# Clipping a block's tap results on VectorE instead of ScalarE, in a deformable bottleneck followed by a batch-norm bottleneck

## The chip, the cores and the metric

The kernel runs on one core of a Trainium2 chip. The metric is the device time of one execution in microseconds; lower is better. TensorE (PE in the profile), VectorE (DVE), ScalarE (ACT) and GpSimd (POOL) each work through a queue of instructions in order, and SyncE (SP) issues most of the DMAs. PEld is TensorE's loading of weights, which overlaps its matmuls.

## The reference, cut to what matters

```python
def _L0_conv_ref(x, w1, b1, w_off, b_off, w2, b2, w3, b3):     # x: (4, 1024, 56, 56) float32
    r = jax.nn.relu(_conv(x, w1, b1))                          # 1x1, 1024 -> 256
    r = jax.nn.relu(_deform_conv3x3(r, w2, b2, w_off, b_off))  # 9 taps, 256 -> 256
    r = _conv(r, w3, b3)                                       # 1x1, 256 -> 1024
    return jax.nn.relu(x + r)

def _deform_conv3x3(feat, w, b, w_off, b_off):
    off = _conv(feat, w_off, b_off)                            # an offset for each pixel and tap
    ...
    sampled = _bilinear_gather(feat, ys.reshape(n, -1), xs.reshape(n, -1))
    out = jnp.einsum('nckhw,ock->nohw', sampled, w.reshape(w.shape[0], c, K))
    return out + b[None, :, None, None]
```

A second bottleneck follows (1x1, 3x3 and 1x1 convolutions with batch norm over all images), and its result is added to its input. The change lies in the first one: in the bias `b` and the relu behind `_deform_conv3x3`.

## The kernel before, in words

All data is float32. An image of 56 x 56 pixels is cut into seven blocks of 512, 512, 512, 512, 384, 384 and 320 pixels (`SIZES`), so four images have 28 blocks, and a block has nine taps.

**The tap stage** (about 210 to 2050 us of the span) is one loop over the 252 taps of all blocks. In each turn of the loop, three things are recorded for three different taps:

- `sample`, two taps ahead: for each 128 pixels, GpSimd issues an indirect DMA that gathers four neighbours (L509), ScalarE scales the first (L519) and VectorE adds the other three (L521). The gathered tiles `g` have eight buffers.
- `turn`, one tap ahead: TensorE transposes the sampled pixels (L546), ScalarE copies them out of PSUM (L552) and VectorE makes three differences (L554, L555, L556). These feed a product of 2 x 2 blocks in seven multiplications.
- `tap`: the seven matmuls (L574), summed over the nine taps in four banks of PSUM.

Behind a block's ninth tap, `tap` copies the seven sums out with five instructions on ScalarE (L589 to L593) and joins them with seven additions on VectorE (L595 to L601). The result is `r2`, a tile of two halves of 128 channels with a row of the block's pixels each. One turn of the loop later, `clip_taps` adds the bias and applies the relu on ScalarE, in place, one instruction for each half (L609), and puts the block on the list `last_ones`.

What is left of TensorE's time in a turn goes to other stages, as generators that give way after each piece: `stage_a` of a later image (first 1x1 convolution L331, seeds L283, offsets L421, the table for the gathers L394) and `stage_c` of a finished block taken from `last_ones`. `stage_c` seeds a bank with the input (L632, ScalarE), multiplies `r2` (L636), applies the relu into `x1t` (L647, ScalarE) and feeds that into the first convolution of the second bottleneck (seeds L283 and L658, matmuls L662, copy out L672). A budget of TensorE columns per turn decides how much of these is recorded behind each tap. A scheduler then settles each engine's own order; an engine executes that order strictly.

For the last image, a further generator, `filters`, prepares the second bottleneck's 3x3 weights on VectorE (L724 to L736 and L777). Behind the tap stage come the 3x3 convolution (to about 2380 us) and the last 1x1 convolution with the output (to the end).

Of the kernel before, what the change touches and what calls it, by code (L numbers as in the profile page):

```python
# [10 lines left out]
AF = mybir.ActivationFunctionType  # L11
ALU = mybir.AluOpType
# [4 lines left out]
KB = CB // 128  # L17
# [17 lines left out]
SIZES = (512, 512, 512, 512, 384, 384, 320)  # L35
# [26 lines left out]
def deform_bottleneck_then_bn_bottleneck(  # L62
# [15 lines left out]
    nc = tc.nc  # L78
# [25 lines left out]
    def col(name, k):  # L104
        c = COLS[name] + k
        return ch[:, c : c + 1]
# [66 lines left out]
    with ExitStack() as l0:  # L173
# [327 lines left out]
        samples, turned, accs, r2s = {}, {}, {}, {}  # L501

        def sample(n, j, k):

            size = SIZES[j]
            for t in range((size + 127) // 128):
                m = min(128, size - t * 128)
                g = gat.tile([128, 4 * CB], F32, tag="g", name=f"g_{n}_{j}_{k}_{t}")
                nc.gpsimd.indirect_dma_start(  # L509
                    out=g[:m],  # L510
                    out_offset=None,
                    in_=tables[n].rearrange("r q c -> r (q c)"),
                    in_offset=bass.IndirectOffsetOnAxis(
                        ap=idxs[n, j][:m, t, k : k + 1], axis=0
                    ),
                )
                s = w3p.tile([128, CB], F32, tag="s", name=f"s_{n}_{j}_{k}_{t}", bufs=8)
                wt = wts[n, j][:m, :, t, k : k + 1]
                nc.scalar.activation(s[:m], g[:m, 0:CB], AF.Copy, scale=wt[:, 0])  # L519
                for corner in range(1, 4):  # L520
                    nc.vector.scalar_tensor_tensor(  # L521
                        s[:m],
                        g[:m, corner * CB : (corner + 1) * CB],
                        wt[:, corner],
                        s[:m],
                        ALU.mult,
                        ALU.add,
                    )
                samples[n, j, k, t] = s

        def turn(n, j, k):

            size = SIZES[j]
            half = size // 2
            sts = w3p.tile([128, 7, 256], F32, tag="sts", name=f"sts_{n}_{j}_{k}", bufs=2)
            banks = [
                ps1.tile([128, 512], F32, tag="bank", name=f"stp_{n}_{j}_{k}_{h}")
                for h in range(KB)  # L540
            ]
            for t in range((size + 127) // 128):
                m = min(128, size - t * 128)
                s = samples.pop((n, j, k, t))
                for h in range(KB):
                    nc.tensor.transpose(  # L546
                        banks[h][:, t * 128 : t * 128 + m],
                        s[:m, h * 128 : (h + 1) * 128],
                        ident[:m, :m],
                    )  # L550
            for h, to in ((0, sts[:, 0:3:2, :half]), (1, sts[:, 3:5, :half])):
                nc.scalar.copy(to, banks[h][:, :size].rearrange("p (e q) -> p e q", e=2))  # L552
            t1, t2 = sts[:, 2, :half], sts[:, 1, :half]
            nc.vector.tensor_sub(t1, t1, sts[:, 0, :half])  # L554
            nc.vector.tensor_sub(t2, sts[:, 4, :half], t1)  # L555
            nc.vector.tensor_sub(sts[:, 5:7, :half], sts[:, 1:4:2, :half], sts[:, 0:2, :half])  # L556
            turned[n, j, k] = sts
# [4 lines left out]
        def tap(n, j, k):  # L562
            size = SIZES[j]
            half = size // 2
            if k == 0:
                accs[n, j] = [
                    pst.tile([128, 512], F32, tag=f"tap{i}", name=f"acc2_{n}_{j}_{i}")
                    for i in range(4)
                ]
            sts = turned.pop((n, j, k))  # L570
            sums = [accs[n, j][i // 2][:, i % 2 * half : (i % 2 + 1) * half] for i in range(7)]
            for i, (a, b) in enumerate(PRODUCTS):

                nc.tensor.matmul(  # L574
                    sums[i],
                    w2[:, a, k],
                    sts[:, b, :half],
                    start=(k == 0 and i % 2 == 0),
                    stop=(k == TAPS - 1),
                    skip_group_check=True,  # L580
                )
            if k == TAPS - 1:
                r2 = work.tile([128, KB, 512], F32, tag="r2", name=f"r2_{n}_{j}", bufs=R2S)
                p3, p5, p4 = (
                    w3p.tile([128, CB], F32, tag="p", name=f"p{i}_{n}_{j}", bufs=3)[:, :half]
                    for i in (3, 5, 4)
                )
                r = [[r2[:, o, e * half : (e + 1) * half] for e in range(2)] for o in range(KB)]
                nc.scalar.copy(r2[:, 0, :size], accs[n, j][0][:, :size])  # L589
                nc.scalar.copy(p3, sums[2])  # L590
                nc.scalar.copy(p5, sums[3])
                nc.scalar.copy(r2[:, 1, :size], accs[n, j][2][:, :size])
                nc.scalar.copy(p4, sums[6])  # L593
                add = nc.vector.tensor_add
                add(r[1][0], r[1][0], r[0][0])  # L595
                add(r[1][1], r[1][1], r[1][0])
                add(r[0][0], r[0][0], r[0][1])
                add(r[0][1], r[1][0], p5)
                add(r[0][1], r[0][1], p3)
                add(r[1][0], r[1][1], p4)  # L600
                add(r[1][1], r[1][1], p5)  # L601
                r2s[n, j] = r2

        def clip_taps(n, j):

            size = SIZES[j]
            r2 = r2s[n, j]
            for o in range(KB):
                nc.scalar.activation(  # L609
                    r2[:, o, :size], r2[:, o, :size], AF.Relu, bias=col("a_b2", o)  # L610
                )
            last_ones.append((n, j))

        def stage_c(n, j):

# [85 lines left out]
        def last_positions(n):  # L701
            for j in range(NJ - positions_behind(n), NJ):
                yield from stage_b(n, j)
# [271 lines left out]
        last_ones = []  # L975
# [29 lines left out]
        stage, upcoming, extra, done, budget = None, None, None, None, 0.0  # L1005
        for i, (n, j, k) in enumerate(taps):
            if i + 1 < len(taps):
                turn(*taps[i + 1])
            nxt = next(ahead, None)
            if nxt is not None:  # L1010
                sample(*nxt)
            tap(n, j, k)
            if done is not None:
                clip_taps(*done)
            done = (n, j) if k == TAPS - 1 else None
            if (j, k) == (0, 0):
                waiting = last_positions(n) if n else None

            if waiting and k % 2 == 0:
                next(waiting, None)  # L1020
            if (n, j, k) == (N - 1, 1, 0):
                l0a.close()
                extra = filters()
            if extra and k:
                next(extra, None)
            budget += share * SIZES[j]
            passed = (STARTS[j] + SIZES[j] * k / TAPS) / HW
            while budget > 0 or due(n, j, k):
                if stage is None:
                    stage = upcoming  # L1030
                    if stage is None:
                        stage = next_stage(n, j, passed)
                        if stage is None:
                            break
                    else:
                        upcoming = None
                cost = next(stage, 0)
                if cost == LAST:
                    upcoming = next_stage(n, j, passed)
                    if upcoming is not None:  # L1040
                        next(upcoming)
                elif cost == 0:
                    stage = None
                elif cost in (None, BEGUN):
                    if not due(n, j, k):
                        break
                else:
                    budget -= cost
        clip_taps(*done)
        while last_ones or stage or upcoming:  # L1050
            if stage is None:
                if upcoming is None and len(last_ones) == 1:
# [19 lines left out]
    with l1:  # L1072
# [37 lines left out]
        size = (HALF + 2) * KB * W  # L1110
# [291 lines left out]
        for i, p in [(i, p) for i in range(len(parts)) for p in SEQ] + [(len(parts), None)]:  # L1402
            begun = begin(i, p) if p is not None else None
            if before is not None:
                j, q, _ = before
# [71 lines left out]
    with ExitStack() as l2:  # L1477
# [45 lines left out]
        done = 1  # L1523
        before = None
        for i in range(0, len(chunks), 2):
            n, at, m = chunks[i + 1]
# [92 lines left out]
    def add(t, k, e, ps):  # L1619
        to = t[:, e * BLK : (e + 1) * BLK]  # L1620
        nc.vector.scalar_tensor_tensor(to, ps, sc3[:, k : k + 1], to, ALU.mult, ALU.add)  # L1621
# [170 lines left out]
```

## Time and profile before

| what | value |
|---|---|
| time of the runs, median of 3 | 2801.86 us (2799.9 to 2802.9) |
| the profiled execution's own time | 2791.22 us |
| its span, first to last instruction | 2789.4 us |
| mean granted TensorE clock | 0.992 of full speed |
| busy: TensorE, VectorE, ScalarE, GpSimd | 2722.1, 2183.5, 1496.3, 1169.8 us |
| L609, the clip on ScalarE | 56 instructions, 545 to 752 ns each |
| L521, VectorE's sums of samples | 2700 instructions, 1173.8 us |

A group of instructions is named by line, engine, operation and `out<-in` tiles, with its shape and count, then its busy time in us, the mean of one in ns, and the idle time of the engine just before it with what ended that. A wait reads "engine tile line <- who ended it: total us, times, longest us". A row of the timeline gives start, duration, engine, line, operation, tiles and count; in brackets stands the idle time before it and its releaser. A row of windows gives a stretch of the span and each engine's busy time in it.

### The profile page before, as it was taken

How to read it: one execution, taken by the hardware profiler on the slowest of the kernel's cores; microseconds unless marked ns; L12 is line 12 of the kernel's file. 1: busy time of each engine (PE TensorE's matmuls, PEld its weight loads, DVE VectorE, ACT ScalarE, POOL GpSimd, SP SyncE). 2: the span in 40 equal slices, each digit the busy share in tenths (PEclk: the TensorE clock that was granted, in tenths of full speed). 3: DMA queues.
4: the chain of work that ended last, by engine and by line, in shares of the span. 5: the costliest groups of instructions: out<-in, count | busy, mean ns of one | idle time of the engine just before them, and what ended most of it. 6: DMA issues, size and time to landing. Idle time of an engine off the chain costs nothing.

```text
span 2789.4 us, 39697 instructions
## 1 busy us (share of the span) xinstructions
PE 2722.1 (98%) x12045; PEld 1927.4 (69%) x12045; DVE 2183.5 (78%) x5199; ACT 1496.3 (54%) x3045; POOL 1169.8 (42%) x1054
## 2 busy tenths in 40 slices
PE   9989999999999999999999999999989999999999
PEld 7656666777666676667676666667769999864554
DVE  5488888888788889877788989878759988337777
ACT  2345656565545655556565656666643444524444
POOL 0166554565665466556555656554500000111111
PEclk9999999999999999999999999999999999999999
DMA  8699999999999999999998989999831110219998
GB/s 291 203 344 387 367 350 327 314 338 353 352 334 349 349 291 350 314 344 369 338 345 278 375 296 351 343 368 341 269 123 38 36 43 5 95 60 341 347 346 304
DMA packets 313318, 792.70 MB, mean 284 GB/s; under 512 B 33768, under 2 KB 134672, under 8 KB 313104
## 3 DMA queue, kind: packets, MB, share of 16 engines
q0 software_dynamic: 127296, 462.48, 46.6%
q1 hardware_dynamic: 167376, 276.30, 28.7%
q10 hardware_dynamic: 18432, 51.39, 4.7%
q8 instruction: 95, 1.56, 0.2%
q14 instruction: 119, 0.97, 0.1%
HBM read 640.94 MB, written 143.75 MB: 281 GB/s over the span
## 4 chain that ended last, share of the span: by engine, by line
PE 85%; DVE 6%; DMA 5%; ACT 2%; issue 1%; SPq 1%; ACTq 0%; POOL 0%; DVEq 0%
PE acc L574 21%; PE acc L662 12%; PE pr L636 11%; PE acc L331 8%; PE q L1223 7%; PE stp L546 6%; PE u L1673 3%; DVE s L521 3%; PE acc_g L1505 2%; PE c L1673 2%; PE v L1673 2%; PE pm L421 2%; PE b L1223 2%; DMA g<-table,idxs 2%; PE acc L867 1%
## 5 line engine op out<-in xcount | busy, mean ns | idle before, releaser
L509 POOL DMA_INDIRECT g<-table,idxs x900 | 1096.4, 1218 | 914.8 <-DVE s L521 228.9
L521 DVE SCALAR_TENSOR_TENSOR s<-g,wts,s 128x256 f32<-128x256 f32 (+1 forms) x2700 | 1173.8, 477 | 258.0 <-ACT s L519 125.4
L574 PE MATMUL acc<-sts,w 128*128 128x256 f32 (+2 forms) x3528 | 723.0, 355 | 3.7 <-ACT sts L552 1.2
L574 PEld LDWEIGHTS acc<-sts,w 128*128 128x128 f32 x3528 | 602.9, 191 | 55.7 <-ACT sts L552 4.1
L519 ACT ACTIVATE s<-g,wts 128x256 f32<-128x256 f32 x900 | 425.6, 511 | 215.2 <-PE stp L546 85.3
L636 PE MATMUL pr<-r,w 128*128 128x512 f32 (+2 forms) x896 | 366.7, 546 | 11.0 <-ACT pr L632 6.9
L662 PE MATMUL acc<-x1t,c1w 128*128 128x512 f32 (+2 forms) x896 | 360.8, 545 | 9.1 <-ACT acc L283 7.3
L546 PEld LDWEIGHTS stp<-ident,s 128*128 128x128 f32 (+1 forms) x1800 | 212.3, 141 | 126.7 <-issue 90.8
L331 PE MATMUL acc<-xt,w 128*128 128x448 f32 x704 | 283.4, 544 | 6.7 <-DMA xt<-in_x_dram 6.7
L662 PEld LDWEIGHTS acc<-x1t,c1w 128*128 128x128 f32 x896 | 168.4, 191 | 149.8 <-issue 100.0
L636 PEld LDWEIGHTS pr<-r,w 128*128 128x128 f32 x896 | 166.0, 192 | 143.6 <-issue 86.8
L552 ACT COPY sts<-stp 128x512 f32<-128x512 f32 (+2 forms) x504 | 241.0, 528 | 22.7 <-PE stp L546 17.7
L546 PE MATMUL stp<-ident,s 128*128 128x128 f32 (+1 forms) x1800 | 248.8, 273 | 3.9 <-DVE s L521 3.1
L647 ACT ACTIVATE x1t<-pr,ch 128x512 f32<-128x512 f32 (+2 forms) x224 | 141.8, 633 | 140.8 <-PE pr L636 118.7
L331 PEld LDWEIGHTS acc<-xt,w 128*128 128x128 f32 x704 | 131.8, 192 | 111.0 <-issue 108.6
L1624 ACT ACTIVATE x1f<-x1f,sh_bn 128x896 f32<-128x896 f32 x112 | 116.0, 1041 | 150.9 <-DVE x1f L1621 132.2
L672 ACT COPY y<-acc 128x512 f32<-128x512 f32 (+2 forms) x112 | 59.4, 530 | 216.8 <-PE acc L662 200.8
L556 DVE TENSOR_TENSOR sts<-sts 128x512 f32<-128x512 f32 (+2 forms) x252 | 155.3, 616 | 0.8
L632 ACT COPY pr<-xr 128x512 f32<-128x512 f32 (+2 forms) x224 | 121.5, 542 | 3.8
L1621 DVE SCALAR_TENSOR_TENSOR x1f<-u,sc_bn,x1f 128x448 f32<-128x448 f32 x156 | 106.6, 683 | 18.9 <-PE u L1673 9.4
L1223 PE MATMUL q<-v,u 128*128 128x196 f32 x576 | 108.5, 335 | 8.5 <-DVE v L1175 7.7
L554 DVE TENSOR_TENSOR sts<-sts 128x256 f32<-128x256 f32 (+2 forms) x252 | 97.5, 387 | 23.2 <-ACT sts L552 21.5
(298 smaller groups left out, 3042.5 us busy)
## 6 DMA issues: line engine op xcount, KB each, us to landing
xt<-in_x_dram SPq DMA_DIRECT2D x112, 448.0 KB
x1f<-x_d SPq DMA_DIRECT2D x96, 448.0 KB
out_dram<-x1f ACTq DMA_DIRECT2D x96, 448.0 KB
xr<-in_x_dram SPq DMA_DIRECT2D x128, 256.0 KB
x_d<-x1t SPq DMA_DIRECT2D x128, 256.0 KB
table<-ft SPq DMA_DIRECT2D x56, 384.0 KB
g<-table,idxs POOLq DMA_INDIRECT x900
xr<-in_x_dram SPq DMA_DIRECT2D x64, 192.0 KB
```

The source lines that it names most:

```text
L331: nc.tensor.matmul(acc, w1[:, k, h * 128 : (h + 1) * 128], xts[n, j, k - k % 2][:, k % 2, :], start=start, stop=(k == KC - 1), skip_group_ ...
L509: nc.gpsimd.indirect_dma_start(out=g[:m], out_offset=None, in_=tables[n].rearrange("r q c -> r (q c)"), in_offset=bass.IndirectOffsetOnAxi ...
L519: nc.scalar.activation(s[:m], g[:m, 0:CB], AF.Copy, scale=wt[:, 0])
L521: nc.vector.scalar_tensor_tensor(s[:m], g[:m, corner * CB : (corner + 1) * CB], wt[:, corner], s[:m], ALU.mult, ALU.add,)
L546: nc.tensor.transpose(banks[h][:, t * 128 : t * 128 + m], s[:m, h * 128 : (h + 1) * 128], ident[:m, :m],)
L552: nc.scalar.copy(to, banks[h][:, :size].rearrange("p (e q) -> p e q", e=2))
L556: nc.vector.tensor_sub(sts[:, 5:7, :half], sts[:, 1:4:2, :half], sts[:, 0:2, :half])
L574: nc.tensor.matmul(sums[i], w2[:, a, k], sts[:, b, :half], start=(k == 0 and i % 2 == 0), stop=(k == TAPS - 1), skip_group_check=True,)
L636: nc.tensor.matmul(z, w3[:, h, k * 128 : (k + 1) * 128], r2[:, h, :size], start=False, stop=(h == KB - 1), skip_group_check=True,)
L662: nc.tensor.matmul(z, c1w[:, k, h * 128 : (h + 1) * 128], x1ts[k], start=False, stop=(i == KC // 2 - 1), skip_group_check=True,)
L1223: nc.tensor.matmul(ps[:, o].rearrange("p r c -> p (r c)"), wt, x, start=first and j == 0 and (alone or o == 0), stop=last and j == len(pai ...
L1673: nc.tensor.matmul(to, wt, x, start=start, stop=stop, skip_group_check=True)
```

## The change

`clip_taps` is gone. Right behind the seven additions, still inside `tap`, two VectorE instructions add the bias and take the maximum with zero, in place. The block joins `last_ones` at the same turn of the loop as before, so `stage_c` takes it up at the same place.

```diff
@@ tap
                 add(r[0][1], r[0][1], p3)
                 add(r[1][0], r[1][1], p4)
                 add(r[1][1], r[1][1], p5)
+
+                for o in range(KB):
+                    nc.vector.tensor_scalar(
+                        r2[:, o, :size], r2[:, o, :size], col("a_b2", o), 0.0,
+                        op0=ALU.add, op1=ALU.max,
+                    )
                 r2s[n, j] = r2
-
-        def clip_taps(n, j):
-
-            size = SIZES[j]
-            r2 = r2s[n, j]
-            for o in range(KB):
-                nc.scalar.activation(
-                    r2[:, o, :size], r2[:, o, :size], AF.Relu, bias=col("a_b2", o)
-                )
-            last_ones.append((n, j))
@@ the loop over taps, and once behind it
-                clip_taps(*done)
+                last_ones.append(done)
```

More of the change, by code (lines that the diff above doesn't have):

```diff
@@ L1048, in deform_bottleneck_then_bn_bottleneck @@
                     budget -= cost
-        clip_taps(*done)
+        last_ones.append(done)
         while last_ones or stage or upcoming:
```

## The prediction

> **What bounds the kernel now.** I read the page first: its engine totals, then the chain that ended last, then the waits of PE (the tensor engine), then the timeline around the one place where the moved instruction holds something up.
>
> ```profile
> PE 2722.1 (98%) x12045; PEld 1927.4 (69%) x12045; DVE 2183.5 (78%) x5199; ACT 1496.3 (54%) x3045; POOL 1169.8 (42%) x1054
> PE 85%; DVE 6%; DMA 5%; ACT 2%; issue 1%; SPq 1%; ACTq 0%; POOL 0%; DVEq 0%
> ```
>
> PE is busy for 2722.1 of 2789.4 us and carries 85% of the chain. The change adds no matmul, so it can give back no more than PE's idle time, 67.3 us in the whole span, and it costs only where it opens a new gap on PE. Of these gaps, the ones in the tap stage (about 210 to 2050 us) that end on ScalarE (ACT) are in the waits of PE:
>
> ```profile
> PE acc L662 <- ACT acc L283: 7.3, 3, 4.0
> PE pr L636 <- ACT pr L632: 6.9, 4, 4.3
> PE pr L636 <- ACT r L609: 4.0, 1, 4.0
> ```
>
> Columns: total us, times, longest. L609 is the clip that moves. In its own name it held PE once, for 4.0 us. What it did to others is in the waits of ACT and in the timeline of the tap stage's late part:
>
> ```profile
> ACT r L609 <- DVE r L599: 30.9, 15, 8.9
> ...
> 1641.78 0.72 ACT L609 ACTIVATE r<-r,ch 128x512 f32<-128x512 f32 x1 [8.94 <-DVE r L599]
> 1642.41 0.56 ACT L647 ACTIVATE x1t<-pr,ch 128x384 f32<-128x384 f32 x1
> 1642.87 0.71 ACT L609 ACTIVATE r<-r,ch 128x512 f32<-128x512 f32 x1
> 1643.48 0.57 ACT L283 ACTIVATE acc<-zero_col,ch 128x384 f32<-128x384 f32 x1
> ...
> 1644.11 3.64 PE L662 MATMUL acc<-x1t,c1w 128*128 128x384 f32 x6 [4.04 <-ACT acc L283]
> ```
>
> ACT stood 8.94 us at L609, because VectorE (DVE) was late with its sums (DVE itself had waited 8.35 us for a DMA at L724). Behind L609 in ACT's queue were x1t L647 and the seed L283, which PE needed: PE lost 4.04 us. So the largest of the three L283 waits belongs to the clip too.
>
> **What the Trainium skill says.** "VectorE: DVE Perf Modes", section "The perf-mode tier table", gives an fp32 tensor_scalar in SBUF two elements a cycle and a tensor_tensor one. The trace agrees: tensor_scalar takes 414 ns for 512 columns (L777) and 547 for 768 (L736), 0.52 ns a column; tensor_tensor takes 417 for 256 (L598) and 683 for 512 (L556), 1.04. "SBUF — State Buffer", section "SBUF: two separate sides", says that such a two-port operation shares an exclusive lock with GpSimd, so that descriptors of a gather are not written meanwhile. The trace fits: the gather issue at 1660.82, with three L736 inside it, took 3.39 us, while the commonest take 0.94; but the one before it took 3.12 without any, so the size isn't proved. "Perfetto Trace Analysis", section "Optimizing Scalar/DVE Operations", advises moving work to ScalarE if DVE is saturated; here the move goes the other way, onto the busier engine (78% against 54%).
>
> **The change part by part.**
>
> ```profile
> L609 ACT ACTIVATE r<-r,ch 128x512 f32<-128x512 f32 x32 | 23.1, 722 | 25.7 <-DVE r L599 24.5 <-issue 0.6 <-DVE r L601 0.3
> L609 ACT ACTIVATE r<-r,ch 128x384 f32<-128x384 f32 x16 | 9.9, 618 | 4.9 <-DVE r L599 4.8
> ...
> L777 DVE TENSOR_SCALAR u<-u 128x512 f32<-128x512 f32 x3 | 1.2, 414 | 0.0
> L1595 DVE TENSOR_SCALAR sc_bn<-sc_bn,sp 128x8 f32<-128x8 f32 x1 | 0.2, 222 | 0.0
> L1591 DVE TENSOR_SCALAR mom<-mom 128x8 f32<-128x8 f32 x1 | 0.2, 171 | 0.0
> ```
>
> Removed: 56 activations on ACT, 23.1 + 9.9 + 8 x 0.55 = 37.4 us, and the 30.9 us that ACT stood before them. All but the two places above lies beside PE work, so 68 us less on ACT is worth 4 us.
>
> Added: 56 tensor_scalars on DVE. 414 ns for 512 columns, 348 for 384 and 320 for 320 by 0.52 ns a column; a per-partition scalar costs 51 ns more (222 against 171 on 128x8). So 465, 399 and 371 ns: 32 x 0.465 + 16 x 0.399 + 8 x 0.371 = 24.2 us. Lower bound without the 51 ns: 21.4. Upper bound, if the in-place form ran at one element a cycle (683 + 51 for 512, 600 and 533 for the others): 37.4. I take 24.2, since the trace's other SBUF tensor_scalars run at the double rate. DVE goes from 78 to 79% busy.
>
> Moved: in the built order the first clip stands between L600 and L601 and the second right behind L601 or one row later. No wait is added on DVE, since both read what DVE itself wrote. Queued behind them are the next tap's sample sums L521 and differences L554 to L556, then the gather that needs a buffer which L521 frees. Each block's end makes these about 0.8 us later (two clips, each 0.08 less than its duration, as rows of DVE overlap by that much). In some ends the built order also puts two or three L521 ahead of L554 (block 0,2): 1.6 us in all. SP's and POOL's queues keep their DMAs; one xr load passes two others. PE's order changes in one place, in the second image's first blocks, by five rows.
>
> What covers this: I paired the timeline's rows of L554, L555 and L556 with the matmuls L574 that read them, over 252 taps. They end a median 6 us before PE comes to them, and in nine taps of ten over 3.3. The second tap after a block's end, the first to feel the clips, has 1.9 us at least. So 0.8 us is hidden by PE's queue. It is not where DVE never rests:
>
> ```profile
> 1050.00:1120.00 70.00, 69.21 (x312) 46.60 (x312) 65.88 (x184) 40.60 (x90) 48.47 (x37) 1.00 0.96 354
> 1540.00:1610.00 70.00, 70.00 (x298) 46.39 (x297) 66.66 (x193) 47.31 (x98) 45.09 (x38) 1.00 1.00 373
> ```
>
> Columns: the stretch, its length, then busy us of PE, PEld, DVE, ACT and POOL. DVE has 4.1 and 3.3 of 70 us left; 0.8 us stays on for 44 and 51 us, and the thinnest cover there is 0.6 and 1.0 us. Cost 0 to 0.4 us: I take 0.3. The gather's issue may be stretched by up to 2.5 us (3.39 less 0.94) at a block's end; the same 6 us cover it, cost 0, or the rival below.
>
> The 1640 stall: ACT is free from 1632.84, so the seed and x1t are ready by about 1635, and PE runs L662 when its taps end, at 1640.07. Next late is DVE: L521 of the second-next tap ended at 1645.66, the built order makes it 1646.3, and PE would want it at 1640.07 + 5.67 = 1645.7, the last two of eight transposes at 1646.5. So 3.8 of 4.04 us go; bounds 2.5 and 4.0.
>
> The end of the stage: PE waited 4.02 us for the last block's clip at 2040.26. That wait isn't removed, only its releaser changes. L599 to PE was 1.03 us; on DVE the first clip starts when L600 is through, about 2039.8, and lasts 0.37, so PE starts between 0.1 earlier and 0.2 later. Cost 0.
>
> Sum: -3.8 + 0.3 + 0 = -3.5 us on the profiled execution's own 2791.2 us (span 2789.4 and 1.8 around it): 2787.7. The median of the runs shown, 2801.9, stands 10.6 higher, and I carry that over: 2798.4 us.
>
> **The rivals.** *ACT's relief reaches further.* All PE waits on ACT in the tap stage are 7.3 + 6.9 + 4.0 + 2.1 + 1.5 + 1.2 + 1.7 (three small ones), 24.7 us. Against it: of the long ones, 4.28 us at 1677 stood behind a late gather and 2.09 at 1135 behind a late DMA of offsets, not behind the clip. Half of the rest might go: -10 us, 2792. *DVE's delay comes through.* If clip, reordering and a stretched gather add up (0.8 + 0.8 + 2.5 = 4.1 us) they pass the cover at the block's ends where it is thin. It decides where a tap's cover is under 4 us; that is so within the next four taps behind 8 of 27 ends. Eight times 1.5 us is 12: 2801.9 - 3.5 + 12 = 2810.4. For it: DVE at 94% in two stretches, and the start of the taps, where around 222 us PE's weight loads already wait for L521. Against it: the median cover of 6 us. *It doesn't do what it says:* the scheduler keeps PE's order, PE never sees ACT's time, and the 1640 stall only changes its name, since DVE's 8.35 us wait at L724 stays: 2801.9.
>
> **How the numbers follow.** About 0.2%, 5.6 us, is what a measurement of this kernel can tell from no change. My forecast has 0.52, and with an uncertainty of 3 us about a quarter of it lies beyond -5.6. The far-reaching relief has 0.11, the delay 0.22, no effect 0.15. Faster 0.13 + 0.11 = 0.24; slower 0.21; within 0.2%, 0.55. The range takes in most of both rivals: 2790 to 2812. The likeliest case alone is 2795 to 2802.
>
> **What would show it.** In the changed profile: no L609 on ACT and ACT near 1459 us busy; 56 tensor_scalars of about 465, 399 and 371 ns on DVE, 2208 us busy; no wait of PE on L283 over 2.5 us, and PE idle about 64 us. Durations near 734 ns would show the single rate. A longer list of PE waits on DVE's L521 and L554 to L556, over 10 us in all, would make the forecast wrong, and so would gathers whose mean issue grows well over 1218 ns.

## The result and the profile after

| | before | after |
|---|---|---|
| runs of the first comparison, median | 2800.38 us (19 runs) | 2805.85 us (19 runs) |
| ratio, 95% interval | | 1.0021 [1.0011, 1.0031] |
| profiled execution, own time / span | 2791.22 / 2789.4 us | 2802.86 / 2801.1 us |
| TensorE idle in the whole span | 67.3 us | 78.5 us |

The change costs about 0.2% in this comparison, where 3.5 us less was forecast. The median lies inside the stated range of 2790 to 2812 us, but in the part that the range owed to a rival (VectorE's delay comes through), not to the likeliest case. Two more comparisons of the same pair, told below, gave 1.0012 and 0.9992. So the loss is small, and over the three comparisons it is not clear of no change.

The engine totals and the chain by engine, from the page of the kernel after:

```profile
PE 2722.6 (97%) x12045; PEld 1928.8 (69%) x12045; DVE 2199.9 (79%) x5255; ACT 1466.3 (52%) x2989; POOL 1181.7 (42%) x1054
PE 81%; DMA 8%; DVE 6%; ACT 3%; issue 1%; SPq 1%; ACTq 0%; DVEq 0%; POOLq 0%
```

TensorE is as busy as before to 0.5 us. The two spans differ by 11.7 us, and 11.2 of them are idle time of TensorE. On the chain, 4 points moved from PE, most of them to DMA (5% before). The clips, from the groups by form:

```profile
L604 DVE TENSOR_SCALAR r<-r,ch 128x512 f32<-128x512 f32 x32 | 15.4, 481 | 0.0
L604 DVE TENSOR_SCALAR r<-r,ch 128x384 f32<-128x384 f32 x16 | 6.8, 428 | 0.0
L604 DVE TENSOR_SCALAR r<-r,ch 128x320 f32<-128x320 f32 x8 | 3.0, 381 | 0.0
```

The waits of PE over the span (total us, times, longest); L632, L658 and L628 are the lines that were L636, L662 and L632 before:

```profile
PE pr L632 <- ACT pr L628: 12.3, 7, 5.3
PE acc L331 <- DMA xt<-in_x_dram: 9.7, 2, 6.9
PE acc L658 <- ACT acc L283: 8.1, 4, 2.5
...
PE stp L546 <- DVE s L521: 6.7, 9, 1.3
...
PE pr L632 <- DVE r L604: 3.9, 1, 3.9
```

The 4.04 us wait for a seed L283 at 1644 is gone: the longest L283 wait is now 2.5. But the waits for ScalarE's seeds of `pr` rose from 6.9 to 12.3 us, with one of 5.3 that was not there. It stands at 1702.52, and the timeline of POOL, ACT and PE ahead of it is the key to this case:

```profile
1681.32 12.65 POOL L509 DMA_INDIRECT g<-table,idxs  x1 [0.30 <-ACT s L519]
1681.38 0.96 DVE L724 SCALAR_TENSOR_TENSOR u<-ends 128x768 f32<-128x768 f32 x1
...
1686.29 0.51 ACT L519 ACTIVATE s<-g,wts 128x256 f32<-128x256 f32 x1 [2.34 <-DMA g<-table,idxs]
...
1687.31 2.86 DVE L521 SCALAR_TENSOR_TENSOR s<-g,wts,s 128x256 f32<-128x256 f32 x7
...
1694.28 0.94 POOL L509 DMA_INDIRECT g<-table,idxs  x1 [0.30 <-issue]
...
1697.47 0.51 ACT L519 ACTIVATE s<-g,wts 128x256 f32<-128x256 f32 x1 [7.20 <-DMA g<-table,idxs]
...
1701.99 0.48 ACT L628 COPY pr<-xr 128x384 f32<-128x384 f32 x1
...
1702.52 2.93 PE L632 MATMUL pr<-r,w 128*128 128x384 f32 x4 [5.26 <-ACT pr L628]
```

One gather took GpSimd 12.65 us to issue; the next took 0.94. Inside the long issue VectorE ran sums, differences and the weights of `filters` (L724, L729, L732) and rested only in the last 0.8 us. ScalarE stood 7.20 us at L519 for the late data. Behind L519 in its queue was L628, a seed that needs no gather, and TensorE was waiting for that seed. The wait is booked on ScalarE, while its cause lies two queues away.

### The profile page after: what moved, and what is told of

The parts are those of the page before. It is cut to its first block, busy times and chain, and to the rows that moved or that the text cites. A ratio compares the mean times of both kernels' runs of the same rounds, so it can differ in the third digit from the quotient of the medians.

```text
span 2801.1 us, 39749 instructions
## 1 busy us (share of the span) xinstructions
PE 2722.6 (97%) x12045; PEld 1928.8 (69%) x12045; DVE 2199.9 (79%) x5255; ACT 1466.3 (52%) x2989; POOL 1181.7 (42%) x1054
## 4 chain that ended last, share of the span: by engine, by line
PE 81%; DMA 8%; DVE 6%; ACT 3%; issue 1%; SPq 1%; ACTq 0%; DVEq 0%; POOLq 0%
PE acc L574 20%; PE acc L658 11%; PE pr L632 10%; PE acc L331 9%; PE q L1219 6%; PE stp L546 6%; DMA g<-table,idxs 5%; PE u L1669 4%; DVE s L521 3%; PE acc_g L1501 2%; PE c L1669 2%; PE v L1669 2%; PE pm L421 2%; PE b L1219 2%; PE acc L863 1%
## 5 line engine op out<-in xcount | busy, mean ns | idle before, releaser
L509 POOL DMA_INDIRECT g<-table,idxs x900 | 1108.2, 1231 | 913.5 <-DVE s L521 264.9
L521 DVE SCALAR_TENSOR_TENSOR s<-g,wts,s 128x256 f32<-128x256 f32 (+1 forms) x2700 | 1176.3, 479 | 265.2 <-ACT s L519 255.8
L574 PE MATMUL acc<-sts,w 128*128 128x256 f32 (+2 forms) x3528 | 720.2, 355 | 3.6 <-ACT sts L552 1.2
L574 PEld LDWEIGHTS acc<-sts,w 128*128 128x128 f32 x3528 | 601.7, 190 | 54.3 <-ACT sts L552 5.2
L519 ACT ACTIVATE s<-g,wts 128x256 f32<-128x256 f32 x900 | 428.5, 511 | 267.4 <-DMA g<-table,idxs 121.4
L632 PE MATMUL pr<-r,w 128*128 128x512 f32 (+2 forms) x896 | 366.4, 546 | 16.2 <-ACT pr L628 12.3
L658 PE MATMUL acc<-x1t,c1w 128*128 128x512 f32 (+2 forms) x896 | 361.2, 546 | 8.2 <-ACT acc L283 8.1
L331 PE MATMUL acc<-xt,w 128*128 128x448 f32 x704 | 284.6, 546 | 9.7 <-DMA xt<-in_x_dram 9.7
L658 PEld LDWEIGHTS acc<-x1t,c1w 128*128 128x128 f32 x896 | 169.2, 192 | 147.6 <-issue 96.1
L632 PEld LDWEIGHTS pr<-r,w 128*128 128x128 f32 x896 | 165.5, 192 | 148.7 <-issue 83.7
L331 PEld LDWEIGHTS acc<-xt,w 128*128 128x128 f32 x704 | 132.2, 192 | 113.4 <-issue 107.8
L556 DVE TENSOR_TENSOR sts<-sts 128x512 f32<-128x512 f32 (+2 forms) x252 | 155.5, 617 | 0.3
L628 ACT COPY pr<-xr 128x512 f32<-128x512 f32 (+2 forms) x224 | 121.5, 542 | 3.9
L554 DVE TENSOR_TENSOR sts<-sts 128x256 f32<-128x256 f32 (+2 forms) x252 | 97.6, 387 | 13.7 <-ACT sts L552 13.4
```

Source lines behind the costliest of these rows:

```text
L331: nc.tensor.matmul(acc, w1[:, k, h * 128 : (h + 1) * 128], xts[n, j, k - k % 2][:, k % 2, :], start=start, stop=(k == KC - 1), skip_group_ ...
L509: nc.gpsimd.indirect_dma_start(out=g[:m], out_offset=None, in_=tables[n].rearrange("r q c -> r (q c)"), in_offset=bass.IndirectOffsetOnAxi ...
L521: nc.vector.scalar_tensor_tensor(s[:m], g[:m, corner * CB : (corner + 1) * CB], wt[:, corner], s[:m], ALU.mult, ALU.add,)
L574: nc.tensor.matmul(sums[i], w2[:, a, k], sts[:, b, :half], start=(k == 0 and i % 2 == 0), stop=(k == TAPS - 1), skip_group_check=True,)
L632: nc.tensor.matmul(z, w3[:, h, k * 128 : (k + 1) * 128], r2[:, h, :size], start=False, stop=(h == KB - 1), skip_group_check=True,)
L658: nc.tensor.matmul(z, c1w[:, k, h * 128 : (h + 1) * 128], x1ts[k], start=False, stop=(i == KC // 2 - 1), skip_group_check=True,)
```

## The experiments

"Late form" means VectorE clips recorded one turn later, where ScalarE's clips stood. The first set asked whether VectorE's added work at a block's end costs the time, or ScalarE's changed order (B), or a lock by which VectorE's two-port operations keep GpSimd from issuing (C). From the second set on, P is the changed order of TensorE behind the first block, and Q the place of the clips right behind the sums in every block.

**e1_no_clip.** The five lines of the new loop are taken out of the changed kernel.

> Leaves out the bias and the relu behind the tap sums on both engines (56 instructions fewer on ScalarE, none more on VectorE). Its ScalarE order differs from before in the same places as the changed kernel's (24 rows moved against 27). Theory A, VectorE's 24 us of clips late in its queue are the loss: ratio to before 0.998 to 1.000, the 1640 stall of PE gone. Theory B, the new ScalarE order (L519, which waits for gathers, moved ahead of copies and seeds) is the loss: ratio about 1.002, and the 1640 stall replaced by waits of PE on ScalarE's L628 and L283 behind L519, over 18 us in all. Theory C, the two-port clips lock GpSimd's gather issue: as A, and the gather issues' mean at or under before's 1218 ns.

0.9985 [0.9975, 0.9996]. So neither ScalarE's relief nor its reordering, which this kernel all but shares with the changed one, loses time. A kernel with no clip on any engine is only some 4 us faster than before.

**e3_dve_late.** `clip_taps` as before, with the engine exchanged:

```diff
-                nc.scalar.activation(
-                    r2[:, o, :size], r2[:, o, :size], AF.Relu, bias=col("a_b2", o)
-                )
+                nc.vector.tensor_scalar(
+                    r2[:, o, :size], r2[:, o, :size], col("a_b2", o), 0.0,
+                    op0=ALU.add, op1=ALU.max,
+                )
```

> The clip on VectorE as in the changed kernel, but recorded where before had it, one turn of the tap loop later, behind the next tap's differences. VectorE's work is the same as in the changed kernel, only the place moves. Theory A (place in VectorE's queue ahead of the next tap's work): ratio to before 0.999 to 1.000. Theories B and C (ScalarE's order; the port): ratio about 1.002, like the changed kernel.

0.9986 [0.9976, 0.9996], with VectorE as busy (2199.1 us) as in the changed kernel. VectorE's time by itself isn't the loss.

**e4_two_ports_more** and **e5_one_port_more.** The changed kernel with idle VectorE work behind the clips of every block but the last: two-port in the first, one-port in the second (what they write is read by nothing).

```diff
+                if (n, j) != (N - 1, NJ - 1):
+                    for i in range(12):
+                        nc.vector.tensor_scalar_max(p3, r[i % KB][i // 2 % 2], 0.0)
```

```diff
+                if (n, j) != (N - 1, NJ - 1):
+                    for i in range(4):
+                        nc.vector.bn_stats(spent, r2[:, i % KB, :size])
```

> The changed kernel with twelve more tensor_scalars of 128x256 (about 281 ns each) behind each block's clips but the last, reading r2 and writing a spent tile: 91 us more on VectorE, all in the two-port form. Theory C: gather issues grow from 1231 ns to over 1400 in the mean and the ratio to before is over 1.006. Theory A: ratio 1.005 to 1.010, and the run with one-port work of the same length is as slow. Theory B: ratio within 0.001 of the changed kernel's 1.002.

> The changed kernel with four more BATCH_NORM_STATS2 of 128x512 (about 687 ns each) behind each block's clips but the last, reading r2 and writing six spent columns: about 70 us more on VectorE, one source and the single rate, so no two-port form. Theory C: ratio close to the changed kernel's 1.002, gather issues not longer than 1231 ns. Theory A: as slow as the two-port run, 1.005 to 1.010. Theory B: within 0.001 of 1.002.

1.0089 [1.0069, 1.0109] and 1.0206 [1.0189, 1.0224]. VectorE grew by 56 and 55 us. If the clips' own two ports were the cause, e4 would be the worse one; it is much the better, so C in that form falls. A, which expected the two to be equally slow, missed as well. Yet work at this place is dear: e5 stands 2860.51 - 2801.25 = 59 us above before, with 55 us more of VectorE than the changed kernel, on an engine that is 79% busy. Most of it does not show as VectorE's in the waits of PE: those that ended on ScalarE grew from 33.8 us before to 71.7, those that ended on VectorE from 14.3 to 28.0. The longest entry is 19.0 us for `pr` seeds of ScalarE, the next 12.8 for VectorE's L522. The timeline of e5 has the same figure as the kernel after, a hundred us later (L510, L520, L522, L632 and L636 of e5 are L509, L519, L521, L628 and L632 of the kernel after; L611 is the added `bn_stats`):

```profile
1784.65 0.70 DVE L611 BATCH_NORM_STATS2 spent<-r 128x6 f32<-128x512 f32 x1
...
1785.84 6.04 DVE L522 SCALAR_TENSOR_TENSOR s<-g,wts,s 128x256 f32<-128x256 f32 x15
...
1786.30 6.73 POOL L510 DMA_INDIRECT g<-table,idxs  x1 [4.71 <-ACT pr L632]
...
1796.15 0.51 ACT L520 ACTIVATE s<-g,wts 128x256 f32<-128x256 f32 x1 [6.04 <-DMA g<-table,idxs]
...
1798.80 0.51 ACT L520 ACTIVATE s<-g,wts 128x256 f32<-128x256 f32 x1 [2.15 <-DVE s L522]
...
1799.76 0.43 ACT L632 COPY pr<-xr 128x320 f32<-128x320 f32 x1
...
1800.24 2.50 PE L636 MATMUL pr<-r,w 128*128 128x320 f32 x4 [6.65 <-ACT pr L632]
```

While VectorE was at the block's end (until about 1785.8), samples piled up; then it ran 15 sums L522 without a rest. GpSimd, idle for 4.71 us, then began a gather inside this run, and its issue took 6.73 us. ScalarE stood 6.04 us for it and 2.15 us more at the next L520, for a sum, and TensorE lost 6.65 for a seed queued behind both.

**e6_first_late, e7_first_early, e8_stage_c, e2_act_early.** The changed kernel with the first block's clips late and the 27 others early (TensorE's order is before's), the reverse (TensorE's order is the changed kernel's), the VectorE clips at the head of `stage_c`, and the clips on ScalarE right behind the sums. The edit of e6, whose `clip_taps` serves block (0, 0) alone; e7 has the two conditions exchanged:

```diff
-                for o in range(KB):
-                    nc.vector.tensor_scalar(...)
+                if (n, j) != (0, 0):
+                    for o in range(KB):
+                        nc.vector.tensor_scalar(...)
```

> The clip on VectorE: for the very first block one turn late, as in the late run, for the other 27 blocks right behind the sums, as in the changed kernel. TensorE's built order is then that of before in every row; the changed kernel's differs from it in one place, behind the first block. Theory P (the loss is that one change of TensorE's order, where a matmul that needs a load still in flight stands ahead of the offsets' matmuls and transposes): ratio to before 0.9985 to 0.9995, as in the late run. Theory Q (the loss is the clips' place ahead of the next tap's differences in all blocks): ratio 1.001 to 1.002, as in the changed kernel.

> The reverse: the first block's clips right behind its sums, those of the other 27 blocks one turn late. TensorE's built order is the changed kernel's. Theory P: ratio to before 1.001 to 1.002, and PE waits about 2.8 us for the load xt near 228 us, which the late run doesn't. Theory Q: ratio 0.9985 to 0.9995.

> The clip on VectorE, recorded at the start of stage_c of its block, its only reader, so as late as it can be; TensorE's order is that of before. Theory Q: at least as good as the late run, ratio 0.997 to 0.9985. Theory P: the same as the late run, 0.9985 within 0.001.

> The clip stays on ScalarE but is recorded right behind the sums, where the changed kernel has it. TensorE's order isn't the changed kernel's (it differs from before elsewhere, by four transposes in the third image). Theory Q, in the form that the place right behind the sums is bad for whoever clips there: ratio to before 1.001 to 1.004, ScalarE's wait for L599 over 30.9 us. Theory P: 1.000 within 0.001.

0.9990 [0.9973, 1.0007], 0.9985 [0.9973, 0.9997], 0.9988 [0.9976, 0.9999] and 0.9983 [0.9971, 0.9995]. All expectations of a loss missed: Q's for e6 and e2, P's for e7. Neither shows at the clips' own size, and this set can't decide between P and Q: the times differ by less than the comparison tells. Hence a larger load, and the measurement itself.

**e10_after_again, e11_before_again, e12_late_again**, and on another chip **e19_after_third, e20_late_third.** Copies.

> The changed kernel as it stands, once more, beside before, before's own copy and the late form. Theory Q (the clips right behind the sums push back the sums and weights of the next sample; no single block does it): 1.001 to 1.003 of before, and 0.15 to 0.3% above the late form on the same chip. Theory R (a difference of 0.2% between two builds belongs to the sample of runs as much as to the program, since all four variants of the second set came out 0.1 to 0.2% below before): 0.999 to 1.0005 of before, and within 0.1% of the late form.

> The kernel before, measured as if it were a variant: what the comparison shows when nothing is changed. If the comparison is fair to 0.1%, 0.999 to 1.001. If it has a bias against the kernel that is called before (which would explain that every light variant so far stands at 0.998 to 0.999), about 0.9985, and then all ratios near there are to be read as no change, and 1.0021 as a loss of some 0.35%.

> VectorE clips, recorded one turn later, where ScalarE's clips stood; TensorE's order is before's. It was 0.9986 of before in the first set. Theory Q: again 0.998 to 0.9995, and 0.15 to 0.3% below the changed kernel. Theory R: anywhere from 0.998 to 1.001, and within 0.1% of the changed kernel.

> The changed kernel a third time: 1.001 to 1.002 of before if the loss belongs to the program (1.0021 and 1.0012 so far); within 0.0005 of 1 if the first comparison was an outlier.

> The late form a third time (0.9986 and 1.0007 so far): 0.999 to 1.000. Theory Q: the changed kernel's median is 2 to 6 us above this one. If the place does not matter at the size of the clips, they stand within 1.5 us of each other.

| kernel | ratios to before, in order | weighted by their intervals |
|---|---|---|
| after | 1.0021, 1.0012 [0.9996, 1.0028], 0.9992 [0.9975, 1.0008] | 1.0013 |
| late form | 0.9986, 1.0007 [0.9994, 1.0020], 0.9979 [0.9961, 0.9997] | 0.9991 |
| before against itself | 0.9994 [0.9979, 1.0009] | |

The first and third interval of the changed kernel do not overlap, and those of the late form hardly do. So a single ratio is good to about 0.15% here, not to its interval, and with such a scatter the 1.0013 of three is not clear of 1. On the two chips that ran both, the changed kernel's median stands above the late form's by 2808.14 / 2805.73 = 1.0009 and 2802.20 / 2800.62 = 1.0006. That is the sign of Q each time, and no proof of it: Q had asked for 0.15 to 0.3% in the first pair and for 2 to 6 us in the second, where 1.6 us were found.

**e9_heavy_late.** The late form with e5's four `bn_stats` behind its clips, in `clip_taps`.

> The late form with the same four idle bn_stats a block (2.05 us of VectorE, 27 blocks) that cost 2.06% when they stood right behind the sums (beside the changed kernel). They stand behind the clips, so one turn later; TensorE's order stays before's. It enlarges the difference in place tenfold. Theory Q (the place right behind the sums is what costs, since there the next sample's sums queue behind it): much cheaper late, 1.000 to 1.008, TensorE's waits on VectorE and on the results of taps near those of the late form. If only VectorE's time counts and not its place: 1.016 to 1.022, as early. If the changed order of TensorE in the first block was a good part of the early form's cost: between the two, with the stretches behind 500 us as in the early form.

1.0124 [1.0104, 1.0145], against e5's 1.0206. Place matters, but the late place isn't free either, and Q expected at most 1.008.

**e17_heavy_first_late, e18_heavy_first_early.** e6 and e7 with the four `bn_stats` at the place of each block's clips.

> Clips on VectorE and the four idle bn_stats a block right behind the sums in all blocks but the first, whose clips and load stand one turn later; TensorE's order is before's. All early was 1.0206 of before, all late 1.0124. Theory Q (the place costs in every block alike): 1.018 to 1.022. Theory P (the changed order of TensorE behind the first block, and the staggering of work that follows from it, makes the difference): 1.010 to 1.014.

> The reverse: clips and load right behind the sums in the first block alone, one turn later in the other 27; TensorE's order is that of the all-early heavy kernel. Theory Q: 1.010 to 1.014. Theory P: 1.018 to 1.022. If the two add up, both of these stand near 1.0165.

1.0196 [1.0161, 1.0231] and 1.0108 [1.0069, 1.0146]. At this load this decides for Q and against P: with TensorE's order of before and all blocks but the first early, the cost is that of all early; with TensorE's order of e5 and one block early, it is that of all late. The stretch of the tap stage, 205 to 2055 us, in windows of e17 and then of e18 (length, busy time of PE, matmuls, granted clock, share of the DMA engines, GB/s):

```profile
205.00:2055.00 1850.00, 1782.79 (x7666) 0.98 0.91 328
```

```profile
205.00:2055.00 1850.00, 1806.88 (x7862) 0.99 0.93 332
```

TensorE rests 1850 - 1782.8 = 67.2 us in e17's and 43.1 us in e18's. For comparison, the kernel after and before:

```profile
205.00:2055.00 1850.00, 1817.29 (x7938) 0.99 0.94 333
```

```profile
205.00:2055.00 1850.00, 1825.96 (x7980) 1.00 0.94 333
```

32.7 and 24.0 us: 8.7 of the 11.7 us between the two profiled executions lie in this stage.

**e21_nine_early, e22_nine_late.** e5 and e9 with a ninth buffer for gathers, in case a late release of buffers was what delayed them. The room comes from the identity's loads `xr`, which have three buffers in place of five:

```diff
-        xres = l0.enter_context(tc.tile_pool(name="xres", bufs=5))
-        gat = l0.enter_context(tc.tile_pool(name="gat", bufs=8))
+        xres = l0.enter_context(tc.tile_pool(name="xres", bufs=3))
+        gat = l0.enter_context(tc.tile_pool(name="gat", bufs=9))
```

> The all-early heavy kernel (1.0206) with nine buffers for gathers in place of eight; the room comes from the identity's loads, three buffers in place of five. Theory G (the block's end holds back the sums that free the gathers' buffers, the next gathers are issued late, and ScalarE stands at L520 for them): ScalarE's wait for gathers falls from 230 us below 190, and the time to 1.010 to 1.015, unless the fewer buffers of the identity cost as much, which the late twin shows. Theory D (VectorE's own sums and weight sets are late to TensorE, whatever the gathers do): 1.018 to 1.024, and the gap to the late twin stays 0.6 to 1.0%.

> The all-late heavy kernel (1.0124) with the same nine and three buffers. Both theories: 1.008 to 1.014; above 1.016 the fewer buffers of the identity cost. What counts is its distance from the early twin: under 0.3% by theory G, 0.6 to 1.0% by theory D.

1.0177 [1.0151, 1.0202] and 1.0137 [1.0119, 1.0156]. ScalarE's wait for gathers fell from 229.7 to 127.7 us as theory G had it, but the time did not fall to 1.015, and the gap of 0.4% lies between the two theories. In the profiled pair the gap in TensorE's idle time did not close at all (58.5 against 34.6 us in the tap stage; 66.5 against 45.3 with eight buffers). The number of buffers is a part at most.

**What goes with the loss.** From the timeline of POOL, I counted the gather issues of over 4 us between 200 and 2100 us in every profiled execution, and set TensorE's idle time of 205 to 2055 us beside them (1850 less the busy time of the windows):

| kernels | issues over 4 us | their sum, us | TensorE idle, us |
|---|---|---|---|
| before, twice | 3, 5 | 15.6, 24.6 | 24.0, 25.6 |
| e1, e2 | 5, 2 | 25.1, 11.1 | 24.1, 25.3 |
| late: e3, e12, e20, and e7 | 3, 3, 3, 3 | 13.8, 15.7, 12.9, 13.5 | 25.2, 28.8, 21.9, 24.1 |
| early: after, e10, e19, and e6 | 4, 8, 3, 6 | 25.5, 36.8, 14.0, 26.7 | 32.7, 33.5, 25.8, 31.9 |
| e8, at `stage_c` | 6 | 31.6 | 31.7 |
| e4 | 11 | 51.6 | 39.9 |
| heavy, late: e9, e18, e22 | 10, 9, 8 | 53.5, 43.1, 39.0 | 45.3, 43.1, 34.6 |
| heavy, early: e5, e17, e21 | 17, 15, 19 | 87.3, 72.8, 98.4 | 66.5, 67.2, 58.5 |

Over the 20 executions the two columns have a correlation of 0.95 (0.77 over the 13 without added load); each us of long issues goes with half a us of idle TensorE. At the clips' own size, too, the four early executions rest 31.0 us in the mean and the four late ones 25.0. Those 6 us, 0.2%, have the sign of the ratios above. All of the difference is in waits that ended on ScalarE: 21.9 us in the mean of the early four, 15.9 in the late four; VectorE's are 5.6 and 5.9. In the heavy kernels ScalarE's are 52.3 us early and 33.5 late. e8 is late and rests 31.7 us: it does not fit the place, but it fits the issues. e19, one of the early ones, has as few long issues as before, as little idle time, and the one ratio of the changed kernel below 1. This is an association over programs, with the chain shown in two places. None of the four long issues of the kernel after has a clip inside it. What turns an issue long is shown in part in the last section.

## Why the prediction was wrong

Its direction of effects was right in part. One step failed, one term was mis-sized, and the range held because of a rival.

- **Clips.** Forecast 465, 399 and 371 ns, measured 481, 428 and 381: the double rate, 25.3 us in place of 24.2. Busy time moved less than these sums, on both engines: VectorE +16.4 us (forecast +24 to 2208), ScalarE -30.0 (forecast -37.4 to 1459). Rows overlap their neighbours: of the 25.3 us of clips, only 16.4 are not covered by other rows of VectorE, and of ScalarE's 37.5, only 29.9. The prediction used that for a block's delay (0.08 us a clip) but not for the totals.
- **The 1640 stall.** The 4.04 us went as forecast, and VectorE was next as forecast, but later: PE waits 0.48 and 1.08 us for L521 at 1649 to 1651, where the forecast left 0.24. So 2.5 us of the 3.8 came, its lower bound, and a new 1.59 us wait for a `pr` seed at 1658.65 takes back more. Even in full, this gain would have been less than the 8.7 us that the stage lost in the profiled pair.
- **The tail.** 4.02 us became 3.9 under VectorE's name, as forecast.
- **TensorE's order.** Costed at nothing. The timeline does show the moved L331 waiting 2.85 us for its load at 228.44, a wait that should have been priced: it is a third of the 8.7 us. It does not decide: e10 and e19, the same kernel, do not have it, and e18 has such a changed order and stands at 1.0108, no worse than e9 without it.
- **The step that failed** is "What covers this": the cover of 6 us, and with it the gather's issue, "stretched by up to 2.5 us [...] the same 6 us cover it, cost 0". Two things were wrong in it. The 6 us were measured on one path alone, from VectorE's differences L554 to L556 to the matmuls L574. A late gather takes another: it stops ScalarE at L519, and seeds that have no data to do with it are queued behind; their cover was never measured. The prediction had such a case in hand, the 4.28 us at 1677 that "stood behind a late gather", and used it only against ScalarE's relief. And 2.5 us came from the commonest issue and one long one in the trace of before, which already held one of 6.26 us at 1696. In the profiled execution the issues have a tail to 12.65 us. The rival "DVE's delay comes through" had the right ingredients (delay, reordering and a stretched gather that add up), but placed the end at a tap's differences. The waits ended on ScalarE: 22.7 us of the tap stage's against 16.8 before without the last clip's 4.0, which changed its name. VectorE's L521 and L554 to L556 held PE for 8.8 us in the whole span, under the alarm of 10.
- **A line read wrongly.** The issue at 1657.39, "3.12 without any" L736, does have one: an L736 stands at 1659.85. So neither of the two issues is one without a two-port operation inside it, and they could not be set against each other.
- **The alarms.** The mean issue of a gather was to grow "well over 1218"; it grew to 1231. Even e5's is 1287. The mean hides 4 to 17 long ones among 900, and these are what counts.
- **The base.** The sum was made on an execution that rested 67.3 us; a second profile of the same program, e11, rested 76.4 with a span of 2801.0. That is as long as the kernel after's 2801.1. The 11.7 us between the first two profiles overstate the change's cost.

What the Trainium skill says was read too narrowly. The prediction took from "SBUF — State Buffer", section "SBUF: two separate sides", that a two-port operation such as the clip locks GpSimd out. The same item also names a VectorE operation with two inputs in SBUF, against a GpSimd operation that reads SBUF. The sums L521 are such (`g` and `s`), and there are 2700 of them against 56 clips. The traces agree in where it happens: 13 of e5's 17 long issues lie across a run of 12 or more L522 without a rest. That the lock is the reason was not isolated: the sums can't be left out without taking away the gathers' use, and many issues inside such runs were short (last section).

The late form, 0.9991 of before over three comparisons, is too near to 1 to be called a gain; the clips on ScalarE right behind the sums (e2) have 0.9983 from one comparison.

## What to carry to other kernels

Cover has to be measured on every path that leaves a delayed engine, and on an in-order queue that includes work which needs nothing from it but stands behind something that does. Where GpSimd issues gathers beside a busy VectorE, look at the longest issues in the timeline, not at their mean, and put added VectorE work where no backlog of sums has to be caught up without a rest behind it. To settle a loss of 0.2%, enlarge the suspected cost and divide it by place: four more instructions a block took the gap between the two places from about 0.1% to 0.8%.

## What the runs showed of the hardware

- Long issues of gathers stand where VectorE doesn't rest, but that alone does not make them long. In the kernel after, between 200 and 2100 us, 457 of 859 issues took under 1.0 us, and VectorE was idle for 38% of that time; four took over 4 us, 25.5 us together, and VectorE was idle for 5%. Yet 282 took 1.0 to 1.5 us with VectorE idle for only 2%.
- The moment at which the issue begins separates them. Take an unbroken run of sums, rows less than 0.02 us apart, with 2.5 us or more of it still ahead when an issue begins. Over the 20 traces, 137 issues began within 0.07 us of a sum's start; 109 of them lasted to the run's end and 0.8 to 1.2 us beyond it. Of 1038 that began later in a sum, 4 did, and 1034 were done within 1.3 us. Of the 109, 74 had waited for a sum just before. One run of e5 has both kinds:

```profile
1703.37 6.02 DVE L522 SCALAR_TENSOR_TENSOR s<-g,wts,s 128x256 f32<-128x256 f32 x15
1703.59 1.07 POOL L510 DMA_INDIRECT g<-table,idxs  x1 [4.62 <-DVE sts L557]
1706.17 4.37 POOL L510 DMA_INDIRECT g<-table,idxs  x1 [1.51 <-DVE s L522]
```

- Such held issues also follow the place of the clips. The early kernels (after, e10, e19, e6) have 4, 5, 4 and 4, the late ones (e3, e12, e20, e7) 1, 0, 2 and 2, before 1 and 2; heavy, 15, 14 and 16 early against 8, 8 and 8 late. e1, with no clip, has 4 and loses nothing, and e19 with 4 stands below 1, so their number alone does not set the time. The 12.65 us issue is not of this kind: it began 0.34 us into a sum.
- Idle time of TensorE was not the whole cost. e17's profiled span is 38.5 us longer than e18's, but only 22.4 us of it is idle time; the same matmuls are busy for 2749.8 against 2733.7 us, at a granted clock of 0.984 against 0.990. More idle time went with slower matmuls; that the stalls themselves lowered the clock was not tested.
